# A planned four-layer kernel: convolution added up in PSUM, GpSimd's largest product in two, fillers for TensorE from the start

## The chip, the core and the metric

The kernel runs on one core of one Trainium2 chip. Its engines work from queues of their own: TensorE (PE; its weight loads are the row PEld), VectorE (DVE), ScalarE (ACT), GpSimd (POOL), and SyncE (SP), whose queue issues the DMAs. The metric is the time of one execution on the device in microseconds. The kernel before takes 1466.25 us (median of three runs, 1457.24 to 1469.72).

## What is computed

Four layers on x, which is 4 batches x 512 tokens x 256 features, all in float32, with a context of the same size. All the layers are wanted in this order:

```python
x = _L0_xattn_ref(x, ctx_1024, mask, ...)      # Mamba2 block, then cross-attention, 8 heads of 32
x = _L1_xattn_ref(x, ctx_1024, ctx_1024, ...)  # cross-attention, 8 heads of 16, and a feed-forward block
x = _L2_xattn_ref(x, ctx_1024, ...)            # cross-attention, 16 heads of 16, gelu
x = _L3_xattn_ref(x, ctx_1024, ...)            # cross-attention, 8 heads of 32, then a recurrence
```

The change touches two places of the Mamba2 block: the causal convolution over time with its silu, and the decay matrix of the scan.

```python
padded = jnp.pad(xBC, ((0, 0), (D_CONV - 1, 0), (0, 0)))
conv = conv_b + sum((padded[:, k:k + L, :] * conv_w[:, k] for k in range(D_CONV)))
xBC = jax.nn.silu(conv)
```

The recurrence at the end of layer 3 is serial over the 512 tokens, for all 4 batches at once, with a state of 64:

```python
def step(s, u_t):
    s = jax.nn.silu(s @ A.T) + u_t
    return (s, s)
```

## The kernel before

**Staging.** Tokens are worked on in four chunks of 128 (c = 0 to 3). A *front* per chunk does the Mamba2 block: projections, the convolution in six groups of 128 channels (`channels`), and a scan per batch (`scan`) that ends in an out-projection (`w_out`). Beside it, keys and values of all four layers are made from the context (`keys`, `slim_keys`, `values`, `of_weights`) and stored to HBM. When all of these are made, `with_keys_made` reuses their memory for the *wide* stream, the attention of layers 0 and 3 (tiles kw, vw, probs_w, turned_w), and loads its parameters. When all scans are done, `with_block_done` reuses the block's memory for the *slim* stream, layers 1 and 2 (tiles ks, vs, topped, probs_s), and loads sixteen parameters. Both streams reload keys and values from HBM for each job of one layer, chunk and batch.

**Rows.** Attention heads are 32 partitions wide, so four of them fit in TensorE's array side by side. A row slot is a group of matmuls that run at once in the array's row groups: two groups from one stream's half, and two more where another thread has a row ready (`rows`, `partner`). With no partner a slot uses half of the array.

**The end.** `from_layer3` makes the recurrence's input u (matmuls with wub). `recurrence` works in bank 7 of PSUM, which it takes for good: per chunk one matmul of u with amat, then per token a matmul into the step's four columns, a Tanh on ScalarE with a product on VectorE, or a Silu on ScalarE alone once all of the wide stream's exponentials are out (`exps["left"] == 0`).

**The planner.** Nothing of the order of work is written out by hand. Every operation is a step of a Python generator, a thread with an urgency; `Flow.run` keeps a planned clock of every engine with a cost for each operation, and emits again and again the operation that can begin first by that plan (a more urgent one if it can begin within 120 ns). What it emits stands in each engine's queue in that order and runs when its semaphores allow. So a change of one cost or one place moves all that follows. As every operation is recorded by the same line (`Op.emit`, line 127), the profile's groups show L127, and are told apart by their tiles.

PSUM has eight banks. `banks.single` gives the free bank whose last reader is planned to be done first, or None; `banks.give` returns one.

**Fillers.** `Flow.fill` looks, before TensorE's next operation, at the planned gap. If it is over 300 ns (GAP), it emits a matmul of ident with ident, whose result nobody reads, as wide as the gap allows, up to 256 columns. In the kernel before, `flow.filler` is set once the last second pass of the slim stream is emitted, so fillers stand only near the end: 184 of them, 168 after the recurrence's last input.

**The convolution.** In `channels`, a projection lands in one bank (px). It is copied to pad, behind the last three columns of the chunk before (halo). The fourth tap and the bias are an affine out of px into the tile xbc in SBUF, after which the bank is given back. Three products on VectorE (`scalar_tensor_tensor`) add the other taps, with both inputs and the output in SBUF. Then a Tanh on ScalarE and a last product make the silu.

**The decay matrix.** `scan` first makes lo, 128 x (8 x 128), as one GpSimd product of a triangle and the step's decay; later two halves of four heads are transformed and multiplied again.

Of the kernel before, what the change touches and what calls it, by code (L numbers as in the profile page):

```python
# [10 lines left out]
AF = mybir.ActivationFunctionType  # L11
ALU = mybir.AluOpType
# [3 lines left out]
P = 128  # L16
# [11 lines left out]
SD = 64  # L28
SZ = SD + 1
# [14 lines left out]
def over(ap, n):  # L44

    p, a = ap.shape
    return ap.unsqueeze(1).to_broadcast([p, n, a])
# [181 lines left out]
class Flow:  # L229
# [100 lines left out]
    def fill(self, e, start):  # L330

        while self.filler is not None and start - e.free > GAP:
            op = self.filler(min(256, int((start - e.free - 80) * 0.3) * 2))
            if op is None:
                return
            begin = max(e.free, self.there([op])) + DRAIN * (e.mode != op.mode)
            if begin + op.cost > start:
                return
            e.mode, e.free = op.mode, begin + op.cost
            op.emit()  # L340
            self.account([op], begin, e.free)
# [113 lines left out]
def tile_kernel(ctx: ExitStack, tc: tile.TileContext, a: dict, out: bass.AP):  # L455
# [509 lines left out]
    def front(c):  # L965
# [28 lines left out]
        def channels(ct):  # L994
            pad = yield Need(pads.take)
            bank = yield on_bank(lambda bank: project_t(ps[:, bank, :], w_in, xt, DI // P + ct))
            px = ps[:, bank[0], :].rearrange("p (b t) -> p b t", b=B)
            yield Until(lambda: halo_from[ct] == c - 1)
            yield G_.tensor_copy(pad[:, :, 0 : NCONV - 1], halo[:, ct])
            yield copy(pad[:, :, NCONV - 1 :], px)  # L1000
            acc = xbc[:, ct, :]
            acc_b = acc.rearrange("p (b t) -> p b t", b=B)
            yield affine(acc_b, px, conv_w[:, ct, NCONV - 1 : NCONV], conv_b[:, ct : ct + 1])
            banks.give(*bank)
            yield G_.tensor_copy(halo[:, ct], pad[:, :, P:])
            halo_from[ct] = c
            for k in range(NCONV - 1):
                yield V.scalar_tensor_tensor(
                    acc_b, pad[:, :, k : k + P], conv_w[:, ct, k : k + 1], acc_b,
                    ALU.mult, ALU.add,  # L1010
                )
            pads.give(pad)
            th = yield Need(ths.take)
            yield A.activation(th, acc, AF.Tanh)
            yield V.scalar_tensor_tensor(acc, th, 1.0, acc, ALU.add, ALU.mult)
            ths.give(th)
            todo["n"] -= 1

# [60 lines left out]
    def scan(c, i, xt, dt, da, dec, xbc, through):  # L1079
# [4 lines left out]
        state = states[i]  # L1084

        lo = yield Need(los.take)
        yield G_.tensor_tensor(lo, over(stri, NH), along(da[:, hh], P), ALU.mult)

        dbx = yield Need(dbxs.take)
        y = yield Need(ys.take)  # L1090
# [262 lines left out]

    us, rs = {}, {}
    fed = set()
    recurred = {"begun": 0, "multiplied": 0}

    def from_layer3(c, b, slot, ct):
        half = b // 2
# [22 lines left out]
    def recurrence():  # L1382
# [7 lines left out]
        for c in range(NT):  # L1390
            yield Until(lambda: {(c, 0), (c, 1)} <= fed)
            h, u, r = hs[c], us[c % 2], rs[c % 2]
            if c == 0:
                own = yield Need(banks.last)
                z = ps[0:SZ, own, :].rearrange("p (t b) -> p t b", b=B)
                yield G_.memset(u[:, :, 0:1], 0.0)
            else:
                yield G_.tensor_copy(u[:, :, 0:1], us[1 - c % 2][:, :, P : P + 1])
# [304 lines left out]
    def slim_second(lo):  # L1703

        for i in range(slim.all):
# [22 lines left out]
                yield from read_both(pr, lambda i, sc: A.activation(p[:, i, :], sc, AF.Exp))  # L1728
                slim_probs[n, lo] = p
            slim.keys_read(job)  # L1730
            if i == slim.all - 1:
                flow.filler = filler

    def slim_weigh():

# [55 lines left out]
        flow.add(job["after"](job["c"], job["b"], ct_slot, ct), CHAIN, f"from {job['l']} {job['c']}")  # L1791

    def filler(n):
        bank = banks.single()
        if bank is None:
            return None
        return mm(
            ps[0:SZ, bank[0], 0:n].rearrange("p (i t) -> p i t", i=2), ident[:, 0:SZ],
            over(ident[:, 0 : n // 2], 2),
        )  # L1800


    def with_keys_made():
# [147 lines left out]
```

## Time and profile before

| | |
|---|---|
| profiled execution | 1469.96 us, span 1468.2 us |
| median of three runs | 1466.25 us |
| mean granted TensorE clock | 0.964 |
| busy: PE, PEld, DVE | 1396.0, 990.9, 912.5 us |
| busy: ACT, POOL | 772.2, 229.8 us |
| fp32 matmul rows | 14656 for 8210 instructions: a float32 matmul is two rows, a transpose one |
| GpSimd's first product of lo, 128x1024 | 16 times, 1956 ns in the mean |
| VectorE's products of the convolution | 72 times, 832 ns in the mean |
| other products on VectorE, 128x512, one input in PSUM | 685 ns |
| filler of 202 columns | 354 ns a row in the mean with the other widths |

Times in the rows are taken by the hardware profiler from one execution. The ends of matmuls are modelled and follow each other in a pipeline, so that a busy TensorE need not be at its peak. In the waits, "A <- B x: t, n, l" means that A stood idle for t us, n times and at most l us, until B's work on x was done. The granted clock is the share of TensorE's full speed that the chip allowed in a stretch.

### The profile page before, as it was taken

The page shows a single profiled execution, that of the slowest core. Times are in us where ns is not written, and L with a number is a line of the kernel's source. Part 1 is how long each engine was busy: PE and PEld are TensorE (multiplying, and loading weights), DVE is VectorE, ACT ScalarE, POOL GpSimd, SP SyncE. Part 2 cuts the span into 40 slices and gives each one's busy share as a digit, 9 for nine tenths or more (in the row PEclk, how much of TensorE's full clock was granted, in tenths as well). Part 3 has the DMA queues.
Part 4 walks back from the last instruction along what each step waited for, and adds up shares of the span by engine and source line. Part 5 has one row for each costly group of instructions (what it writes and reads, how often), then busy time and mean ns, then how long its engine had stood idle before and what let it go on. Part 6 is the DMA issues. An engine that isn't in the chain of part 4 may idle for free.

```text
span 1468.2 us, 34894 instructions
## 1 busy us (share of the span) xinstructions
PE 1396.0 (95%) x14656; PEld 990.9 (67%) x14656; DVE 912.5 (62%) x2084; ACT 772.2 (53%) x1938; POOL 229.8 (16%) x369
## 2 busy tenths in 40 slices
PE   8999999989799999999999999999999999999999
PEld 5666767667475667776667676666767666677555
DVE  5777666666566677577675667666575666667100
ACT  4643434444464566566455656546666554577232
POOL 2244453544100011001010101001010000010000
PEclk9999999999899999899898899999999999999999
DMA  8331212200522122132121122221121231201000
GB/s 247 126 114 47 77 60 82 73 15 30 164 90 91 47 90 90 58 136 75 61 89 39 53 68 95 91 74 62 39 81 62 81 111 47 75 21 40 7 9 15
DMA packets 48245, 107.62 MB, mean 73 GB/s; under 512 B 12820, under 2 KB 24536, under 8 KB 48088
## 3 DMA queue, kind: packets, MB, share of 16 engines
q1 hardware_dynamic: 46584, 105.32, 21.6%
q8 instruction: 115, 1.88, 0.5%
q14 instruction: 42, 0.34, 0.1%
q10 hardware_dynamic: 1504, 0.07, 0.1%
HBM read 85.01 MB, written 20.37 MB: 72 GB/s over the span
## 4 chain that ended last, share of the span: by engine, by line
PE 85%; DVE 7%; ACT 5%; DMA 1%; issue 1%; SPq 0%; POOL 0%; DVEq 0%; ACTq 0%
PE ps L127 85%; DVE tops L127 3%; ACT probs_s L127 2%; DVE xbc L127 1%; ACT probs_w L127 1%; ACT L127 1%; DMA ks<-k 1%; ACT xt L127 0%; DVE h L127 0%; DMA ctx_in<-in_ctx 0%; DVE xt L127 0%; DVE stats L127 0%; DVE top L127 0%; DMA wq<-in_L_xattn_Wq 0%; DVE probs_w L127 0%
## 5 line engine op out<-in xcount | busy, mean ns | idle before, releaser
L127 DVE TENSOR_REDUCE tops<-ps 128x2 f32<-128x1024 f32 (+1 forms) x219 | 235.2, 1085 | 82.1 <-PE ps L127 81.5
L127 ACT ACTIVATE probs_s<-ps 128x1024 f32<-128x1024 f32 (+1 forms) x215 | 193.9, 929 | 101.6 <-PE ps L127 100.3
L127 PE MATMUL ps<-ks,queries 32*128 32x512 f32 x768 | 199.0, 670 | 17.5 <-DMA ks<-k 8.4
L127 PE MATMUL ps<-topped,ks 32*128 32x128 f32 x3072 | 192.4, 297 | 10.1 <-ACT rec_th L127 3.3
L127 PEld LDWEIGHTS ps<-topped,ks 32*128 32x128 f32 x3072 | 159.7, 197 | 35.2 <-issue 10.3
L127 PE MATMUL ps<-ident,probs_w 128*128 128x128 f32 x1024 | 139.8, 282 | 3.1 <-ACT probs_w L127 0.9
L127 PEld LDWEIGHTS ps<-rec,ahalf 65*65 65x65 f32 x656 | 72.9, 142 | 96.4 <-DVE rec L127 28.5
L127 PEld LDWEIGHTS ps<-ident,probs_w 128*128 128x128 f32 x1024 | 118.5, 146 | 20.6 <-issue 8.3
L127 ACT ACTIVATE rec_th<-ps 64x4 f32<-64x4 f32 x328 | 53.6, 163 | 127.2 <-PE ps L127 125.1
L127 ACT COPY turned_w<-ps 128x512 f32<-128x512 f32 x156 | 87.8, 585 | 56.2 <-PE ps L127 53.3
L127 PE MATMUL ps<-kw,queries 32*128 32x512 f32 x512 | 115.6, 641 | 0.8 <-DVE tops L127 0.8
L127 PE MATMUL ps<-probs_s,vs 128*32 128x128 f32 x3072 | 108.9, 283 | 0.7 <-ACT rec_th L127 0.7
L127 POOL COPY rb<-r 128x128 f32<-128x128 f32 x64 | 18.7, 292 | 570.0 <-DVE r L127 434.9
L127 ACT ACTIVATE probs_w<-ps,top 128x512 f32<-128x512 f32 x128 | 87.1, 684 | 27.0 <-DVE top L127 26.9
L127 PE MATMUL ps<-ident 128*65 128x202 f32 (+3 forms) x368 | 99.4, 354 | 0.1
L127 PE MATMUL ps<-rec,ahalf 65*65 65x4 f32 x656 | 88.6, 206 | 7.1 <-DVE rec L127 6.8
L127 ACT ACTIVATE probs_w<-probs_w,top 128x512 f32<-128x512 f32 x128 | 91.5, 717 | 5.4 <-DVE top L127 5.4
L127 PEld LDWEIGHTS ps<-probs_s,vs 128*32 128x32 f32 x3072 | 81.7, 113 | 16.1 <-issue 6.5
L127 DVE TENSOR_REDUCE top<-ps 128x2 f32<-128x1024 f32 (+1 forms) x70 | 78.5, 1125 | 18.3 <-PE ps L127 17.7
L127 DVE COPY turned_w<-ps 128x512 f32<-128x512 f32 x100 | 67.9, 688 | 34.6 <-PE ps L127 33.2
L127 DVE CUSTOM_DVE_ANT_0 probs_w<-ps,masked 128x512 f32<-128x512 f32 x128 | 84.0, 681 | 5.5 <-PE ps L127 5.5
L127 PEld LDWEIGHTS ps<-ks,queries 32*128 32x128 f32 x768 | 58.0, 191 | 41.1 <-issue 18.0
(227 smaller groups left out, 2441.3 us busy)
## 6 DMA issues: line engine op xcount, KB each, us to landing
ks<-k SPq DMA_DIRECT2D x48, 512.0 KB, 4.5
kw<-k SPq DMA_DIRECT2D x32, 512.0 KB, 3.5
vw<-v SPq DMA_DIRECT2D x32, 512.0 KB, 3.7
k<-k_out SPq DMA_DIRECT2D x20, 512.0 KB, 2.6
vs<-v SPq DMA_DIRECT2D x16, 574.0 KB, 3.8
vs<-v SPq DMA_DIRECT2D x16, 302.0 KB, 2.9
v<-v_out SPq DMA_DIRECT2D x8, 512.0 KB, 2.8
v<-v_out SPq DMA_DIRECT2D x4, 574.0 KB, 3.3
```

Source lines behind the costliest of these rows:

```text
L127: return getattr(self.engine.bass, self.name)(*self.args, **self.kw)
```

## The change

Three edits. First, the convolution stays in the projection's bank: the affine and the three products read and write px in place, Tanh reads the bank, the last product writes xbc, and only then the bank is given back. Second, the scan's first product is issued as two, of four heads each. Third, the filler is set before any work is planned, offers several widths, and, if no free bank's filler fits, offers a matmul into partitions 64 to 127 of bank 7 once the recurrence owns it. That last form is entered in the plan as writing nothing.

```diff
     def fill(self, e, start):
 
         while self.filler is not None and start - e.free > GAP:
-            op = self.filler(min(256, int((start - e.free - 80) * 0.3) * 2))
-            if op is None:
-                return
-            begin = max(e.free, self.there([op])) + DRAIN * (e.mode != op.mode)
-            if begin + op.cost > start:
+            n = min(256, int((start - e.free - 80) * 0.3) * 2)
+            for op in self.filler(n):
+                begin = max(e.free, self.there([op])) + DRAIN * (e.mode != op.mode)
+                if begin + op.cost <= start:
+                    break
+            else:
                 return
...
             yield copy(pad[:, :, NCONV - 1 :], px)
-            acc = xbc[:, ct, :]
-            acc_b = acc.rearrange("p (b t) -> p b t", b=B)
-            yield affine(acc_b, px, conv_w[:, ct, NCONV - 1 : NCONV], conv_b[:, ct : ct + 1])
-            banks.give(*bank)
+
+            yield affine(px, px, conv_w[:, ct, NCONV - 1 : NCONV], conv_b[:, ct : ct + 1])
             yield G_.tensor_copy(halo[:, ct], pad[:, :, P:])
             halo_from[ct] = c
             for k in range(NCONV - 1):
                 yield V.scalar_tensor_tensor(
-                    acc_b, pad[:, :, k : k + P], conv_w[:, ct, k : k + 1], acc_b,
-                    ALU.mult, ALU.add,
+                    px, pad[:, :, k : k + P], conv_w[:, ct, k : k + 1], px, ALU.mult, ALU.add
                 )
             pads.give(pad)
             th = yield Need(ths.take)
-            yield A.activation(th, acc, AF.Tanh)
-            yield V.scalar_tensor_tensor(acc, th, 1.0, acc, ALU.add, ALU.mult)
+            yield A.activation(th, ps[:, bank[0], :], AF.Tanh)
+            yield V.scalar_tensor_tensor(
+                xbc[:, ct, :], th, 1.0, ps[:, bank[0], :], ALU.add, ALU.mult
+            )
+            banks.give(*bank)
...
         lo = yield Need(los.take)
-        yield G_.tensor_tensor(lo, over(stri, NH), along(da[:, hh], P), ALU.mult)
+        for j in range(0, NH, 4):
+            h4 = slice(i * NH + j, i * NH + j + 4)
+            yield G_.tensor_tensor(lo[:, j : j + 4, :], over(stri, 4), along(da[:, h4], P), ALU.mult)
...
                 own = yield Need(banks.last)
+                recurred["own"] = True
...
-            if i == slim.all - 1:
-                flow.filler = filler
...
     def filler(n):
+
+        many = [n] + [m for m in (192, 128, 64) if m < n]
         bank = banks.single()
-        if bank is None:
-            return None
-        return mm(
-            ps[0:SZ, bank[0], 0:n].rearrange("p (i t) -> p i t", i=2), ident[:, 0:SZ],
-            over(ident[:, 0 : n // 2], 2),
-        )
+        if bank is not None:
+            for m in many:
+                yield mm(
+                    ps[0:SZ, bank[0], 0:m].rearrange("p (i t) -> p i t", i=2), ident[:, 0:SZ],
+                    over(ident[:, 0 : m // 2], 2),
+                )
+        if recurred["own"]:
+            for m in many:
+                op = mm(
+                    ps[SD:, 7, 0:m].rearrange("p (i t) -> p i t", i=2), ident[:, 0:SD],
+                    over(ident[:, 0 : m // 2], 2),
+                )
+                op.writes = []
+                yield op
...
+    flow.filler = filler
     flow.add(parameters(), CHAIN, "parameters")
```

More of the change, by code (lines that the diff above doesn't have):

```diff
@@ L1355, in tile_kernel @@
     fed = set()
-    recurred = {"begun": 0, "multiplied": 0}
+    recurred = {"begun": 0, "multiplied": 0, "own": False}
     def from_layer3(c, b, slot, ct):
```

## The prediction, made before the changed kernel ran

> **What bounds the kernel now.** I read the chain of waits first, then the slices, then who waits for whom on TensorE, then the granted clock in stretches of 50 and of 3 us.
>
> The chain of work that ended last, shares by engine:
>
> ```profile
> PE 85%; DVE 7%; ACT 5%; DMA 1%; issue 1%; SPq 0%; POOL 0%; DVEq 0%; ACTq 0%
> ```
>
> TensorE carries 85% of it. GpSimd, one of whose products the change splits, has 0%. The slices show how full TensorE is and what clock it was granted:
>
> ```profile
> PE   8999999989799999999999999999999999999999
> ...
> POOL 2244453544100011001010101001010000010000
> PEclk9999999999899999899898899999999999999999
> ```
>
> So there are three kinds of loss: idle TensorE (1468.2 - 1396.0 = 72 us), clock (mean 0.964, that is 0.036 x 1468 = 53 us of clock), and the end, where little work is left. The waits of TensorE (us in total, times, longest):
>
> ```profile
> PE ps L127 <- DMA ks<-k: 8.4, 1, 8.4
> ...
> PE ps L127 <- DMA ctx_in<-in_ctx: 6.7, 1, 6.7
> PE ps L127 <- DVE xbc L127: 5.5, 4, 2.8
> ```
>
> Up to 300 us TensorE waits for the convolution (xbc) only 0.8 us in one place; the other 4.7 us are at 315 to 320. The convolution's own rows, and the clock around one drop (3 us stretches; after the times: busy us of PE, PEld, DVE, ACT, POOL, then clock, DMA share, GB/s):
>
> ```profile
> L127 DVE SCALAR_TENSOR_TENSOR xbc<-pad,conv_w,xbc x72: 653/744/2346, 32.9 to 316.9; 128x512 f32<-128x512 f32 x72
> ```
>
> ```profile
> 606.00:609.00 3.00, 2.05 (x10) 0.70 (x6) 2.98 (x7) 0.00 (x0) 0.00 (x0) 0.80 0.00 0
> 609.00:612.00 3.00, 3.00 (x38) 2.78 (x36) 2.29 (x5) 0.18 (x1) 0.00 (x0) 0.50 0.00 0
> ```
>
> The clock falls to 0.50 for some 10 us although the idle piece just before is 0.95 us long. There are about 17 such drops, most between 400 and 1160 us. The end of the chain in order of time (start, us, what):
>
> ```profile
> 1366.84 21.55 PE ps L127 x160
> 1388.40 73.06 PE ps L127 x518
> ```
>
> The last input of the recurrence is ready at 1366.5 + 0.5; then 41 steps of chunk 2 run alone (21.4 us, 0.52 us a step), then the 128 of chunk 3.
>
> **The change part by part,** against the profiled execution (span 1468.2, execution 1469.96). Numbers on order come from the instruction order of the two built programs.
>
> *Convolution in PSUM.* Same 24 chains, same count. The 72 products took 832 ns in the mean against 653 at best: 72 x 0.18 = 13 us, and 24 x 0.13 = 3 us for the last step, lost where GpSimd held them up. The new form (one input and the output in PSUM) is in no row; nearest are 0.69 us (product with one PSUM input) and 0.81 (affine out of PSUM); I take 0.69, the same operation. ScalarE's affine written to PSUM is in no row either; I keep its 0.78. All of it is hidden behind TensorE, which runs matmuls back to back from 50 to 250 us (3.9 us idle). In return a chain holds its bank past its affine, through three products, tanh and the last step, 3 x 0.69 + 0.63 + 0.69 = 3.4 us longer, two of eight banks at a time; queued behind that are transposes and projections that want a bank. Price 0 to +5; TensorE waited 2.8 us for k_out, a bank's reader, so I take +1.
>
> *GpSimd's product in two.* 16 x 1956 ns become 32; the nearest row, a 128x512 product of the same form on dbx, takes 1081 ns, so +0.2 us a pair, 3.3 us in all. GpSimd is at most 57% busy (28.7 of 50 us at 250 to 300) and off the chain: 0. If that cover were gone, the scan's first matmuls with lo would be late by 0.2 us each time.
>
> *What both do to the order.* The out-projections of the mamba block end after 935 matmuls that are neither fillers nor steps, instead of 1125, while the first rows of the slim streams stay at 1168. Before, the 16 parameter loads stand in SP's queue ahead of the first keys with 43 matmuls to cover them, and TensorE waits 0.9 + 8.4 us. After, 233 cover them: about 104 transposes x 0.108, 18 matmuls x 0.43, 11 row slots x 1.1, 4 weighings x 1.08, some 35 us against 16 us of loading (376.3 to 392.1). With the 4.7 us for xbc that is -14. New is the hand-over: the wide stream now starts with no mamba work beside it. Before, 12.2 us lie between the last weight product (268.1) and the first possible wide row (280.3). Work for about 10 us is at hand there (12 + 8 matmuls x 0.43, 16 transposes x 0.108), then the first rows wait for their maximum and exponential, 4 us: +6, and +3 for a thinner stretch after it. Clock: the two old stalls cost about 8 us of it (0.93 and 0.90 in 300 to 400); I give back 6. Sum -11; ends -20 and +5.
>
> *Fillers at the start.* Nine, before the context lands at 6.7 us. The first 8 transposes took 1.94 us, later ones 1.04, and the matmuls behind them 4.68 instead of 3.7: up to -1.9, and up to +0.9 if the fillers run over. I take -1.
>
> *Fillers all along.* Before the last input of the recurrence there are 101 instead of 16: 9 at the start, 10 at the hand-over, 82 in between, 66 more there than before. At 198 columns one costs 198 x 1.67 ns = 0.33 us (a 256-column one 0.43 when packed). All of it on the path is +22, none is 0; TensorE idles 40 us between 400 and 1350, so I take a third, +7. What waits behind a filler is all of TensorE's queue: 40 of the 82 hold a semaphore wait of their own, 11 of them among the 18 that go beside the recurrence in bank 7. The gain is clock: 40 us of it are lost between 400 and 1350. 27 us of added activity against some 80 us at half clock: -12; ends 0 and -30.
>
> [...]
>
> *Row slots.* 302 instead of 296, those that use half of the array 92 instead of 80: 6 x 1.1 = +6.6.
>
> *The end.* 359 of 511 recurrence steps are multiplied before the last input instead of 342: 17 x 0.52 = -9. TensorE works in order, so this only fails if these steps hold it up earlier; ends -12 and 0.
>
> Sum: -11 + 1 - 1 + 7 - 12 + 6.6 - 9 = -18.4, so 1469.96 - 18.4 = 1451.6. The median of before, 1466.25, is 3.7 under its profiled execution: forecast 1448.
>
> **The rivals.**
> 1. *The clock comes back almost whole.* The drops are set off by little activity, and 82 fillers lift it nearly everywhere: -30 for -12, and none of them late. For it: the drops follow pieces of 0.5 to 1.2 us with one-sided rows and single steps. Against: at 258 to 264 the clock falls with TensorE busy throughout. 1448 - 18 = 1430.
> 2. *The fillers do nothing for the clock,* because the gaps that the schedule counts on are not where the chip has them, or because short gaps don't set the clock: the term of -12 is 0. 1448 + 12 = 1460. [...] The same time results if the new hand-over eats what the removed loading wait gives.
> 3. *Slower: fillers in the way of TensorE's queue, from 400 to 1366.* A filler that waits for a bank's reader, or in bank 7 for the step's own reader, starts when the real matmul could have started. All 66 then cost 0.33: +22 for +7; the clock gains nothing (+12) and twelve more one-sided slots bring about three more drops at 4 us (+12); the hand-over stays uncovered (+5). 1448 + 44 = 1492. With the clock term at 0 the sum passes zero once some 60% of the fillers lie on the path; from there the slots and the hand-over decide. For it: 40 waiting fillers. Against: in the last 73 us of before a filler stands between every two steps, and a step still takes only 0.56 us.
>
> **How the numbers follow.** A measurement of this kernel tells about 1% from no change (its three runs span 0.85%). Faster by more than that is below 1451.6, slower above 1480.9. Forecast 0.44 (its own range, plus and minus 14 for the bounds of the front and the fillers, 1434 to 1462: 0.30 faster, 0.14 same); rival 1 0.18 (faster); rival 2 0.16 (0.02 faster, 0.14 same); rival 3 0.22 (0.02 same, 0.20 slower). Faster 0.50, same 0.30, slower 0.20. The range leaves one tenth on each side: the good end takes in rival 1 and the favourable ends of the front (-9) and of the end (-3), 1418; the bad end takes in rival 2 with all fillers on the path (+15), 1475, and half of what rival 3 lies above that, 1484.
>
> **What would show it.** Right: no wait for ks near 380 us and slim rows at about 380 rather than 392; a bubble of 5 to 10 us at the hand-over; convolution products near 690 ns with hardly a spread; mean clock 0.97 to 0.98; last input to end 92 instead of 102 us. Wrong: a last input later than 1366 with the clock at 0.964 or less (rival 3 if fillers start right at the end of a wait; rival 2 if they lie in real gaps), or TensorE waiting for banks in the first 250 us.

## The result and the profile after

The changed kernel takes 1457.99 us (median of 22 runs, 1449.23 to 1463.28) against 1467.5 us for the kernel before in the same series (22 runs, 1455.82 to 1472.28): ratio 0.9944, 95% interval 0.9923 to 0.9964. It is faster by 0.56%, where 1.25% was forecast (1448 us); it lies inside the range. The profiled execution took 1461.58 us with a span of 1459.9, 8.3 us less than before. The kernel before runs in three groups of times, about 1457, 1464 and 1471 us with granted clocks of 0.974, 0.968 and 0.963, and its profiled execution is of the last group.

The page of the changed kernel: the chain's shares by engine, then the slices.

```profile
PE 87%; DVE 6%; ACT 5%; issue 1%; DMA 1%; POOL 0%; SPq 0%; DVEq 0%; ACTq 0%
```

```profile
PE   9999999999999999999999999999999999999999
...
PEclk9999999999999999999999999989999998999999
```

TensorE is over 90% busy in every slice now, and the five slices with a clock of 0.8 have become two. The waits of TensorE (us in total, times, longest):

```profile
PE ps L127 <- DVE top L127: 5.4, 5, 2.4
PE ps L127 <- ACT rec_th L127: 5.4, 12, 0.6
PE ps L127 <- DVE rec L127: 4.0, 8, 0.8
```

The three loading waits of the matmuls (ks 8.4, ctx_in 6.7, wq 0.9) and the 4.7 us for xbc are gone (fillers now run while ctx_in loads). The first rows of the slim streams start at 386 us, where 392 was the time before and about 380 the forecast. The new hand-over shows as a wait of a filler, in the timeline of TensorE (start, us, operation, in brackets the idle time before it and its releaser):

```profile
354.41 0.65 PE L127 MATMUL ps<-ident 128*65 128x256 f32 x2 [2.36 <-DVE top L127]
```

The products of the convolution (count: shortest/median/longest ns, first and last start) and the end of the chain:

```profile
L127 DVE SCALAR_TENSOR_TENSOR ps<-pad,conv_w,ps x72: 674/750/756, 31.6 to 258.1; 128x512 f32<-128x512 f32 x72
```

```profile
1365.51 12.79 PE ps L127 x94
...
1378.31 74.78 PE ps L127 x518
```

The products have lost their long ones (2346 ns before), and their median is about where it was (744). VectorE's step that makes the last input ready starts at 1365.2 us instead of 1366.5, and 24 steps of chunk 2 are left instead of 41. So of the 8.3 us, 7 are the end, and all that lies before it gave 1.3.

**An account of TensorE.** To see where the rest went I added up the matmul rows of each trace in the order of the instructions: the time from each start to the next, less the idle time in it, and less half of what lay in stretches with a granted clock of 0.50. That splits the span into a lead before the first matmul, *work* at full clock, *idle* time, the *loss* to the half clock (all three up to the last input), and the *end*. It comes to 3 us under the span in each kernel. In us:

| kernel | median | ratio | clock | lead | work | idle | loss | at half clock | end |
|---|---|---|---|---|---|---|---|---|---|
| before | 1467.5 | 1 | 0.964 | 6.7 | 1251.8 | 62.1 | 46.2 | 102 | 98.3 |
| changed | 1458.0 | 0.9944 | 0.975 | 1.4 | 1294.4 | 37.5 | 32.2 | 65 | 91.3 |
| e1 its order, fillers not issued | 1457.0 | 0.9937 | 0.977 | 7.3 | 1274.3 | 49.1 | 30.4 | 61 | 91.2 |
| e2 its order, fillers of 64 columns | 1465.3 | 0.9986 | 0.971 | 1.4 | 1280.5 | 47.7 | 38.6 | 79 | 91.3 |
| e3 edits 1 and 2 | 1468.3 | 1.0012 | 0.969 | 7.2 | 1272.4 | 52.3 | 42.4 | 85 | 95.5 |
| e4 edit 3 | 1447.9 | 0.9879 | 0.990 | 1.4 | 1297.4 | 45.0 | 11.1 | 27 | 86.8 |
| e5 order of e4, not issued | 1469.3 | 1.0033 | 0.966 | 7.3 | 1261.1 | 62.9 | 40.8 | 92 | 89.4 |
| e6 edit 1 | 1475.1 | 1.0072 | 0.968 | 7.3 | 1273.5 | 53.3 | 45.0 | 92 | 88.9 |
| e7 edit 2 | 1491.6 | 1.0186 | 0.956 | 6.9 | 1263.1 | 62.0 | 58.1 | 123 | 95.8 |
| e8 before, NEAR 125 | 1462.3 | 0.9978 | 0.968 | 6.8 | 1254.3 | 59.6 | 38.4 | 85 | 100.0 |
| e9 before, 65 fillers by count | 1461.9 | 0.9984 | 0.986 | 7.2 | 1286.0 | 53.2 | 14.9 | 34 | 99.9 |
| e10 the same over 33 rows | 1499.7 | 1.0242 | 0.958 | 7.3 | 1282.0 | 49.9 | 57.4 | 123 | 98.4 |
| e11 e5, fillers by count | 1469.5 | 1.0037 | 0.986 | 6.9 | 1296.6 | 56.5 | 15.2 | 34 | 89.5 |
| e12 e1, fillers by count | 1478.6 | 1.0103 | 0.978 | 6.9 | 1296.7 | 53.2 | 28.5 | 61 | 89.7 |
| e13 e4, fillers in bf16 | 1454.3 | 0.9959 | 0.975 | 1.3 | 1280.0 | 52.9 | 30.9 | 65 | 89.5 |
| e14 changed, fillers in bf16 | 1456.7 | 0.9958 | 0.974 | 1.3 | 1284.4 | 43.3 | 33.6 | 68 | 91.2 |
| e15 e4, half of the fillers | 1451.4 | 0.9919 | 0.983 | 1.4 | 1279.0 | 56.3 | 18.1 | 41 | 89.5 |
| e16 edits 1 and 3 | 1460.0 | 0.9961 | 0.974 | 1.4 | 1291.7 | 39.7 | 33.2 | 68 | 95.5 |
| e17 edits 2 and 3 | 1453.8 | 0.9899 | 0.988 | 1.4 | 1293.3 | 44.9 | 11.9 | 24 | 98.2 |
| e18 edit 3, NEAR 130 | 1436.2 | 0.9782 | 0.992 | 1.4 | 1286.4 | 42.0 | 8.9 | 21 | 91.1 |

Medians are of the timed runs, all else of one profiled execution each; ratios are against the kernel before on the same chip, worked out from all runs of both, and aren't the quotients of the medians. The profiled executions lie between 2.9 us under (e5) and 6.4 us over (e16) the median of their kernel, so small differences between rows of the account can be the execution's. From before to changed the work grew by 42.6 us: fillers 38.0, row slots 9.4, transposes -4.9, the rest 0. Idle time and lead fell by 29.9, the loss by 14.0, the end by 7.0.

### The profile page after: what moved, and what is told of

It is laid out like the page before. It is cut to its first block, busy times and chain, and to the rows that moved or that the text cites. A ratio compares the mean times of both kernels' runs of the same rounds, so it can differ in the third digit from the quotient of the medians.

```text
span 1459.9 us, 35245 instructions
## 1 busy us (share of the span) xinstructions
PE 1417.6 (97%) x14794; PEld 992.5 (68%) x14794; DVE 910.0 (62%) x2098; ACT 774.3 (53%) x1945; POOL 223.5 (15%) x385
## 4 chain that ended last, share of the span: by engine, by line
PE 87%; DVE 6%; ACT 5%; issue 1%; DMA 1%; POOL 0%; SPq 0%; DVEq 0%; ACTq 0%
PE ps L127 87%; ACT probs_s L127 2%; DVE tops L127 2%; DVE dt L127 1%; ACT L127 1%; DVE top L127 1%; DVE probs_w L127 1%; ACT probs_w L127 1%; DMA ctx_in<-in_ctx 0%; ACT xt L127 0%; ACT turned_w L127 0%; DVE turned_w L127 0%; DVE stats L127 0%; DVE xt L127 0%; DVE h L127 0%
## 5 line engine op out<-in xcount | busy, mean ns | idle before, releaser
L127 PE MATMUL ps<-topped,ks 32*128 32x128 f32 x3072 | 182.7, 296 | 4.9 <-ACT rec_th L127 1.4
L127 PEld LDWEIGHTS ps<-topped,ks 32*128 32x128 f32 x3072 | 150.9, 195 | 28.7 <-issue 11.8
L127 PE MATMUL ps<-ident 128*65 128x202 f32 (+16 forms) x506 | 135.4, 359 | 11.9 <-DVE top L127 4.6
L127 PE MATMUL ps<-ident,probs_w 128*128 128x128 f32 x1024 | 134.1, 276 | 0.4 <-ACT probs_s L127 0.2
L127 PE MATMUL ps<-kw,queries 32*128 32x512 f32 x512 | 124.9, 640 | 1.0 <-ACT rec_th L127 0.6
L127 PEld LDWEIGHTS ps<-ident,probs_w 128*128 128x128 f32 x1024 | 113.8, 142 | 15.5 <-ACT probs_w L127 5.0
L127 ACT COPY turned_w<-ps 128x512 f32<-128x512 f32 x162 | 91.6, 584 | 52.8 <-PE ps L127 49.1
L127 DVE CUSTOM_DVE_ANT_0 probs_w<-ps,masked 128x512 f32<-128x512 f32 x128 | 84.7, 681 | 18.2 <-PE ps L127 18.1
L127 PE MATMUL ps<-rec,ahalf 65*65 65x4 f32 x688 | 92.0, 204 | 0.4
L127 DVE SCALAR_TENSOR_TENSOR rec<-rec_th,ps 64x4 f32<-64x4 f32 x344 | 49.7, 144 | 67.5 <-ACT rec_th L127 62.9
L127 DVE COPY turned_w<-ps 128x512 f32<-128x512 f32 x94 | 63.8, 688 | 25.5 <-PE ps L127 24.0
```

What stands on the lines that cost most here:

```text
L127: return getattr(self.engine.bass, self.name)(*self.args, **self.kw)
```

## The experiments

Letters in an expectation stand for the theories that it names. "Before the end" means before the last second pass of the slim stream is emitted; the fillers after it were left as they are in every kernel. e1, e2, e5 and e9 to e15 change what is issued and not what is planned, so all other work keeps its order.

### The change taken apart: e1 to e8

**e1, fillers planned and not issued.**

```diff
-            op.emit()
+            if self.loud:
+                op.emit()
             self.account([op], begin, e.free)
```

> The changed kernel with its plan untouched, but the 80 fillers from the hand-over to the last input of the recurrence planned and not issued; the nine at the start are left out too, the ones at the end stay. So every other instruction stands in the same order. Three theories. A, fillers are paid for in full (TensorE's account of the changed kernel: 46 us of fillers before the last input against 6.5, idle 37 us against 62): without them TensorE idles about 25 us more, the clock falls from 0.975 to about 0.966, and the time stays within 0.3% of the changed kernel, ratio to before 0.992 to 0.997. B, the clock is worth it: slower than the changed kernel by 10 us or more, ratio 1.000 or above. C, they stand in the way: faster by 10 us or more, ratio 0.988 or below.

1457.03 us, ratio 0.9937 (0.9907 to 0.9966): the time of the changed kernel. Without its fillers the same order had 20 us less work (fillers -36, row slots +9, the rest +7) and 12 us more idle time and 6 of lead. The mean clock of the changed kernel and of e1:

```profile
core 0: 1459.9 us, clock 0.975
```

```profile
core 0: 1455.6 us, clock 0.977
```

A's time came out, but not its clock, which was to fall to 0.966; B and C fell. So in the order of the whole change the issued fillers are worth nothing, and what it gained over before came from the order.

**e2, fillers of 64 columns.** The same kernel with each filler before the end cut to 64 columns when issued.

```diff
-            op.emit()
+            (op if self.loud else self.thin(op)).emit()
```

> The same plan as the changed kernel, but each of the 101 fillers before the last input is issued with 64 columns instead of 198 in the mean (64-column fillers took 0.17 to 0.26 us of TensorE in the changed kernel's trace, the others 0.43 in the mean). A: some 20 us less of filling; if the clock stays near 0.975, TensorE waits instead for about two thirds of it and the ratio to before is 0.988 to 0.994; B: the clock needs the columns, falls to about 0.967, and the ratio is 0.996 or above. C, any filler delays by its own wait, not by its columns: the time stays as the changed kernel's, 0.994.

1465.31 us, ratio 0.9986 (0.9957 to 1.0014), clock 0.971. The 80 short fillers still take 18.6 us of work, 0.23 each, and the half clock grew to 79 us. The ratio is B's (0.996 or above), although B had fallen in e1; A's and C's are missed.

**e3, the first two edits without the third.**

```diff
-    flow.filler = filler
     flow.add(parameters(), CHAIN, "parameters")
```

> The changed kernel with the filler set where the kernel before sets it; 30 fillers before the last input, the rest at the end. Its plan is made anew: 303 row slots, 94 of them half empty, 351 recurrence steps before the last input (before: 296, 80, 342; changed: 302, 92, 359). Under A the gain of the changed kernel is made by the front (-6 us) and the end (9 steps, -5), less the row slots (+7): ratio about 0.997, clock about 0.966. Under B, without the fillers' clock, 1.003 or above. Under C 0.990 or below.

1468.3 us, ratio 1.0012 (0.9984 to 1.0041). Fewer stalls (idle -10) and 9 steps less at the end are eaten by 14 us more in row slots, 94 of them one-sided. The ratio lies between A's 0.997 and B's 1.003 and decides nothing.

**e4, the third edit alone.** The convolution and the GpSimd product as before.

```diff
-            if i == slim.all - 1:
-                flow.filler = filler
...
+    flow.filler = filler
     flow.add(parameters(), CHAIN, "parameters")
```

> The kernel before with the third edit alone (fillers from the start, several widths, bank 7); 115 fillers before the last input, 294 row slots, 76 half empty, 362 steps before the last input. A: the end gives -10 us (20 steps), the fillers and the clock cancel, the loading wait near 380 us stays: ratio 0.991 to 0.995, clock about 0.975. B: 0.985 or below. C: above 1.000.

1447.85 us, ratio 0.9879 (0.9836 to 0.9922): faster than the whole change. The loss fell from 46 to 11 us. The ratio lies between A's and B's; A's clock of 0.975 is missed.

**e5, the order of e4 without the fillers** (the edit of e1).

> The third edit alone gave 1447.9 us (ratio 0.988, granted clock 0.990). This kernel keeps that kernel's order of all other work, and doesn't issue the fillers that lie before the last input of the recurrence (those at the end stay). P (the order that the planner lays out anew sets time and clock, the issued fillers are worth nothing): 1444 to 1452 us, ratio 0.985 to 0.991, clock 0.98 or more. C (the half clock follows windows of 3.41 us in which TensorE idles for about 1 us or more, and the issued fillers empty those windows): idle before the last input rises from 45 to about 60 us, half-clock time from 27 to about 70 us, 1455 to 1464 us, ratio 0.993 to 0.998, clock about 0.970.

1469.31 us, ratio 1.0033 (0.9998 to 1.0068). The mean clock of e4 and of e5:

```profile
core 0: 1444.8 us, clock 0.990
```

```profile
core 0: 1464.7 us, clock 0.966
```

Here the fillers are worth 1.5%: 44 us of filler work against 24 us of idle time and lead, and 30 us of loss. C's time for this kernel was 1455 to 1464; it came out slower, with 92 us at half clock where C had about 70, and P fell. But e1 and e5 are the same edit with opposite results, so "fillers raise the clock" was not yet an explanation.

**e6 and e7, the first and the second edit alone.**

```diff
-        yield G_.tensor_tensor(lo, over(stri, NH), along(da[:, hh], P), ALU.mult)
+        for j in range(0, NH, 4):
+            h4 = slice(i * NH + j, i * NH + j + 4)
+            yield G_.tensor_tensor(lo[:, j : j + 4, :], over(stri, 4), along(da[:, h4], P), ALU.mult)
```

(e7; e6 has the convolution of the change, and near the end the widths that the new filler offers.)

> The kernel before with the first edit alone (the convolution added up in the bank). Both first edits together gave 1468.3 us (ratio 1.0012). Theory G (the convolution's edit brings the front's gain, the split takes it back): 1455 us, ratio 0.992, with the split alone above 1470. Theory N (neither brings anything; what a slim row's slots and an order laid out anew give and take covers both): 1462 to 1473 us, ratio 0.997 to 1.004. In both, the convolution's products take 690 to 760 ns without any over 800.

> The kernel before with the second edit alone (GpSimd's largest product in two). G: above 1470 us, ratio 1.003 or more. N: 1462 to 1473 us, ratio 0.997 to 1.004. The convolution's products on VectorE keep their longest ones over 2 us under both if it is not the size of GpSimd's product that delays them, and fall under 1.3 us if it is.

e6: 1475.1 us, 1.0072 (1.0033 to 1.0112), with products of 675 to 756 ns. e7: 1491.55 us, 1.0186 (1.0138 to 1.0235). Neither theory had a loss from the first edit. e6 has 22 us more work, 12 of it in row slots, against 9 us less idle time and 9 at the end. In the two profiles e6 is only 3 us longer, where the ratio means about 10, so its loss is only in part accounted for. e7 moved the end of the out-projections from 1125 to 1166 matmuls: no idle time less, 11 us more work and 12 us more loss. GpSimd's own rows in e7:

```profile
L127 POOL TENSOR_TENSOR lo<-stri,dt x32: 1034/1040/1489, 67.4 to 351.2; 128x512 f32<-128x512 f32 x32
```

and the longest convolution product fell from 2346 to 1752 ns. The split did what it says, on an engine that has 0% of the chain of before.

**e8, another order and nothing else.**

```diff
-NEAR = 120.0
+NEAR = 125.0
```

> The kernel before with none of the edits, but with the planner's limit NEAR at 125 instead of 120, which only makes it lay out part of the work in another order (72 lone row slots instead of 80). P (any new order moves the time by about as much as the whole change did): beyond 0.3% of the kernel before to either side, that is below 1462 or above 1471 us; by the 8 slots x 1.1 us alone it would be 1458 us. S (an order laid out anew is worth nothing by itself): 1463 to 1470 us, ratio 0.997 to 1.002, clock 0.962 to 0.966.

1462.33 us, ratio 0.9978 (0.9948 to 1.0008): 7 us less by the median, but the interval of the ratio takes in no difference. It leaves P and S undecided; e18 comes back to it.

### What the half clock followed: e9, e10 and the count

In the clock records of before and of the changed kernel 26 stretches at half clock begin and end inside the trace: 8 of 3.413 us, 13 of 6.827, three of 10.240, one of 13.653 and one of 17.067. Those at full clock between them are whole multiples of 3.413 us as well, to 2 ns, so each of the two traces can be cut into one grid of stretches of 3.413 us. In 7 of the 26 cases TensorE was idle for less than 0.1 us in the stretch just before. One of the 7, in the changed kernel (stretch; busy us and rows of PE, PEld, DVE, ACT, POOL; clock; DMA share and GB/s), and TensorE's timeline in it:

```profile
1223.90:1227.30 3.40, 3.40 (x18) 2.24 (x16) 2.98 (x8) 0.22 (x2) 0.00 (x0) 1.00 0.03 5
1227.30:1230.70 3.40, 3.40 (x20) 1.38 (x18) 3.40 (x5) 0.43 (x3) 0.00 (x0) 1.00 0.00 0
1230.70:1234.10 3.40, 3.40 (x10) 1.13 (x10) 2.38 (x6) 0.24 (x2) 0.00 (x0) 0.50 0.00 0
```

```profile
1227.75 0.28 PE L127 MATMUL ps<-rec,ahalf 65*65 65x4 f32 x2
1227.96 1.13 PE L127 MATMUL ps<-ks,queries 32*128 32x512 f32 x4
1229.02 0.28 PE L127 MATMUL ps<-rec,ahalf 65*65 65x4 f32 x2
1229.23 1.13 PE L127 MATMUL ps<-ks,queries 32*128 32x512 f32 x4
```

Busy 3.40 of 3.40 us, and the next stretch runs at 0.50. What fills it are one-sided row slots, 32 rows each in two of the four row groups, and steps of 4 columns. That suggested counting how much of the array works rather than whether TensorE is busy: per matmul row of the trace, columns x rows / 128, spread over its time, and summed over each 3.413 us of the grid. A 256-column filler (two rows of the trace, 0.43 us) counts 512; a one-sided slot counts 512 in 1.1 us (a slot over all four groups took 1.14 us, at 1220.53 us of the changed kernel), so three of them and the steps between them come to about 1500.

I formed this from the traces of before, changed and e1 to e8; e9 to e18 were not there yet. It is a count over the twenty traces of this kernel and its variants; they don't show how the chip decides. Stretches at full clock, and how many of them the half clock follows:

| count in the stretch | first ten traces | followed | e9 to e18 | followed |
|---|---|---|---|---|
| under 1500 | 115 | 113 | 81 | 80 |
| 1500 to 1600 | 34 | 10 | 18 | 7 |
| over 1600 | 3847 | 5 | 3966 | 2 |

The columns of bf16 in e13 and e14 are counted as one half, which was chosen from those two traces (below).

Idle time sorts them far worse: of all 8061 stretches the best single limit on the count (1531) puts 19 on the wrong side, the best limit on idle time 182, and a count that leaves the transposes out 202. Of the 165 stretches (all twenty traces) with over 1 us idle, 90 are followed; 82 of those 90 have a count under 1500, and of the 72 with a count over 1600 only 3 are followed. Of the 47 with under 0.2 us idle and a count under 1500, 46 are followed. 1500 is 1500 / 512 x 0.43 = 1.26 us of the whole array, 37% of the stretch. At half clock the same count goes with what follows: of 175 stretches at half clock with a count under 1500, 174 are followed by another; of 236 over 1600, 32 are. A one-sided slot took 1.13 us at full clock and 2.08 at half clock (1227.96 and 1233.15 us of the changed kernel), so in a stretch at half clock the same work counts about half.

**e9 and e10** test it with the order of before. At places that the trace of before shows as thin (count below 1600 in 3.41 us at any phase) stand 65 fillers of 256 columns, over 128 rows in e9 and over 33 in e10. AT maps the number of a TensorE instruction to the fillers after it (the first entry is shown); they go to bank 7 or to a free bank.

```diff
+AT = {375: 1,
...
+        if e.kind == "PE" and e.after is not None:
+            e.n += 1
+            for _ in range(AT.get(e.n - 1, 0)):
+                e.after(self)
```

```diff
-                dst.rearrange("p (i t) -> p i t", i=2), ident[:, 0 : dst.shape[0]],
-                over(ident[:, :], 2),
+                dst.rearrange("p (i t) -> p i t", i=2), ident[0:33, 0 : dst.shape[0]],
+                over(ident[0:33, :], 2),
```

> The kernel before with its order of all work kept, and 65 fillers of 256 columns by 128 rows put by the position of the instruction, where the trace of before shows stretches of 3.41 us with little work for the array, counted as columns x passes x rows/128. R (the clock halves in the window after one whose count is below about 1530, idle or not; the ten traces so far have 118 of 120 windows below 1516 followed by the half clock and 10 of 3876 above): half-clock time before the last input falls from 102 us to 20 to 40 us, which gives back 30 to 38 us of the 46 us lost to it; the fillers take 65 x 0.43 = 28 us, of which about 10 lie in idle time: 1443 to 1456 us, ratio 0.983 to 0.992, clock 0.983 or more. I (idle time of 1 us and more brings the half clock, busy time of any kind prevents it): only what falls into idle time counts, half-clock time 70 to 90 us, 1462 to 1480 us. Q (the fillers stand in the way): above 1475 us.

> The same kernel as the one before in this list, with the same fillers at the same places and of the same columns, but over 33 rows instead of 128, which takes TensorE as long and counts a quarter. R: half-clock time stays at 75 to 105 us, the fillers' 28 us less some 10 of idle time are paid for without a return: 1472 to 1490 us, ratio 1.003 to 1.015, clock 0.962 to 0.973. I: the same time and clock as with 128 rows, to 0.3%.

e9: 1461.88 us, 0.9984 (0.9956 to 1.0011). e10: 1499.72 us, 1.0242 (1.0206 to 1.0277). The groups of TensorE between 400 and 1350 us by form show that the fillers take the same time (busy us, mean ns of one, idle before), then the slices of the clock, each for e9 and for e10:

```profile
L127 PE MATMUL ps<-ident 128*64 128x256 f32 x86 | 26.3, 414 | 0.2 <-ACT rec_th L127 0.2
```

```profile
L127 PE MATMUL ps<-ident 33*64 33x256 f32 x86 | 27.2, 424 | 0.2 <-ACT rec_th L127 0.2
```

```profile
PEclk9999999999899999999999999999999999999999
```

```profile
PEclk9999999989899999899999899899989999999999
```

Same order, same places, same columns, same occupancy; only the rows differ, and the half clock before the last input goes from 102 us to 34 in the one and to 123 in the other. That is 2.6% in time. I, by which busy time of any kind would do, is refuted. R's clock held in e9; in e10 it fell further than R had it (123 us at half clock against 75 to 105, 0.958 against 0.962 to 0.973). R's time held in neither: e9 was to take 1443 to 1456. Its fillers added 34 us of work, 0.53 each instead of 0.43, and found 9 us of idle time, so they cost nearly what the clock gave back (31 us of loss). e10 lies above R's range: its fillers, too, took 34 us, and it has 20 us more half clock than before without any. Fillers that count a quarter may push other work out of a stretch; no run shows that by itself.

**e11 and e12, fillers by the count in the orders of e5 and e1:** the edit of e9, with AT from the traces of these two (65 and 52 fillers).

> The order of the third edit alone, without its fillers before the last input (1469.3 us, clock 0.966), and 65 fillers of 256 columns put by the position of the instruction where that trace shows a count below 1600 in 3.41 us. R: main part +18 us of filler and shift, half-clock time from 92 to 20 to 40 us (loss 41 to 9 to 18 us): 1445 to 1460 us, ratio 0.985 to 0.996, clock 0.983 or more. I: half-clock time 60 to 80 us, 1465 to 1480 us.

> The order of the changed kernel without its fillers before the last input (1457.0 us, clock 0.977), and 52 fillers of 256 columns put by the position of the instruction where that trace shows a count below 1600 in 3.41 us. The change's own 80 to 100 fillers left 65 us of half-clock time there, about as much as without them. R: 52 x 0.43 = 22 us of filler, 15 us of it on the path; half-clock time from 61 to 15 to 35 us (loss 30 to 8 to 17 us): 1448 to 1460 us, ratio 0.987 to 0.995, clock 0.983 or more. I: half-clock time 50 to 65 us, 1462 to 1475 us.

e11: 1469.49 us, 1.0037 (1.0005 to 1.0069): half clock 92 to 34 us as R had it, and again all of it paid for in work (+35), so that R's time, 1445 to 1460, was missed. Planned into gaps, the fillers of e4 cost 44 us of work and take 18 of idle time and 6 of lead with them; placed by hand, 35 against 6. e12: 1478.6 us, 1.0103 (1.0066 to 1.0139), a miss of R: the half clock stayed at 61 us, in the range of theory I. Stretch by stretch the count holds in e12 too: each of its 8 stretches at full clock with less than 1500 is followed by the half clock. Its thin stretches lie elsewhere than in the trace that they were placed by, several in rows of three or four that begin with 1 us of idle time and then stay at half clock.

### How cheap a filler can be, and which edit holds the change back: e13 to e18

**e13 and e14, the fillers in bf16,** one pass over twice the columns, from a tile of ones made at the start.

```diff
+                op.real = mm(
+                    ps[0:SZ, bank[0], 0 : 2 * m].rearrange("p (i t) -> p i t", i=2),
+                    lit[:, 0:SZ], over(lit[:, 0:m], 2),
+                )
```

> The order of the third edit alone (1447.9 us, clock 0.990), each filler before the end issued as one pass of bf16 over twice the columns (512 instead of 256) instead of two passes of f32: the same columns x passes, and by one pass instead of two about half the time or less. S (columns x passes x rows count, whatever the type): half-clock time before the last input stays at 20 to 45 us; the fillers' 44 us fall to 20 or less, part of it comes back as idle time: 1430 to 1443 us, ratio 0.975 to 0.985, clock 0.983 or more. T (the array's time counts): half-clock time 50 to 90 us, 1445 to 1462 us, clock 0.968 to 0.980.

> The changed kernel (1458 us, clock 0.975; 65 us of half clock with its fillers, 61 without) with its fillers before the end as one pass of bf16 over twice the columns. S: half-clock time as with the f32 fillers, 45 to 70 us, and 10 to 16 us less of TensorE's time on the path: 1442 to 1450 us, ratio 0.983 to 0.989. T: half-clock time 60 to 80 us, 1450 to 1460 us.

e13: 1454.34 us, 0.9959 (0.993 to 0.9987). e14: 1456.68 us, 0.9958 (0.993 to 0.9985). The fillers of e13 take 26.5 us instead of 44 and leave 65 us of half clock instead of 27: T, the array's time counts. e14 lies in T's ranges, too. The two traces have 21 stretches at full clock with such fillers in them and less than 1530 from all else. If a bf16 column counts one half, those that the half clock follows all lie under 1530 and all others over it; if it counts one, about half of those followed lie over it. So here a filler bought clock by its time on the array, and a faster one bought less.

**e15, only the fillers that the count asks for.** The planner keeps the count of its own last 3.41 us.

```diff
-            op.emit()
+            if self.loud or self.lately(e.free) < NEED:
+                op.emit()
```

> The order of the third edit alone, fillers before the end issued only where the plan's own count of columns x passes x rows/128 of the last 3.41 us is below 1800 (57 of 115 are left). If the count is what matters, the 58 others bought nothing but idle time: half-clock time 20 to 45 us, 58 x 0.43 = 25 us less of fillers, some 60% of it on the path: 1432 to 1446 us, ratio 0.976 to 0.988. If the fillers' number matters: half-clock time about 60 us, 1455 to 1462 us.

1451.36 us, 0.9919 (0.989 to 0.9948): no gain over e4. The half clock (41 us) is as the first theory had it, the time lies between both. 25 us less of fillers came back as 11 us of idle time, 7 of loss and 7 of other work.

**e16 and e17, the third edit with the first and with the second:** the changed kernel with GpSimd's product whole again (e16), and with the convolution in SBUF again (e17).

> The changed kernel with the second edit (GpSimd's product in two) undone: first and third edit. The first alone gave 1475 us (1.0072), the third alone 1447.9 (0.988), both and the second 1458 (0.9944). If the first edit's loss (12 us more in slim rows, at full clock) stays beside the fillers: 1452 to 1462 us, ratio 0.991 to 0.997. If the second edit is what takes the gain back: 1440 to 1448 us.

> The changed kernel with the first edit undone: second and third edit. If the second edit's loss alone (24 us) stays beside fillers: about 1470 us, ratio 1.000 to 1.010. If most of that loss is the clock of its order (58 us lost to the half clock against 46 before), which fillers give back: 1445 to 1458 us, ratio 0.985 to 0.995. Its order has 72 lone row slots against 80 before and 349 steps before the last input against 342.

e16: 1460.01 us, 0.9961 (0.9925 to 0.9998), in the range of its first theory. e17: 1453.77 us, 0.9899 (0.9861 to 0.9938), in that of its second. With these the table of the three edits is whole (ratios to before):

| | neither | edit 1 | edit 2 | 1 and 2 |
|---|---|---|---|---|
| without edit 3 | 1 | 1.0072 | 1.0186 | 1.0012 |
| with edit 3 | 0.9879 | 0.9961 | 0.9899 | 0.9944 |

Of these eight only the kernels with the third edit are faster than before. In the whole change that gain comes through the order that the planner lays out with it, since e1 keeps the time without the fillers. The edits don't add up: the first costs 0.7 to 0.8% where the second is absent; beside the second it gains 1.7% without the third edit and costs 0.5% with it. Of what the second costs alone, about half is clock in the trace (12 us of loss, 11 of work), and with the third edit that loss is gone (58 us in e7, 12 in e17).

**e18, the third edit in another order.**

```diff
-NEAR = 120.0
+NEAR = 130.0
```

> The third edit alone with the planner's limit NEAR at 130 instead of 120: another order, with 68 lone row slots instead of 76, 354 steps instead of 362 before the last input and 104 fillers instead of 115. By 8 x 1.1 us less in row slots, 8 x 0.52 us more at the end and 2 us less of fillers: 7 us under the third edit alone, 1441 us, with the clock at 0.985 to 0.990: 1436 to 1447 us, ratio 0.980 to 0.988. If the order's luck with the clock outweighs that: 1450 to 1462 us.

1436.23 us, 0.9782 (0.9747 to 0.9817), 22 us under the changed kernel. Its clock, slices and end:

```profile
core 0: 1432.9 us, clock 0.992
```

```profile
PEclk9999999999999999999999999999999999999999
```

```profile
1338.68 15.51 PE ps L127 x114
1354.19 71.93 PE ps L127 x518
```

The last input is ready 27 us earlier than in the changed kernel and more steps are left after it (the last 128 take 71.9 us, at full clock throughout). Against e4 the work is 11 us less (fillers 6, rows 4), idle 3, loss 2, and the end 4 us longer. It was chosen among 17 settings of the planner's limits for its few one-sided slots, 68, and fewer fillers; how much of the gain is that and how much the luck of one order, one such kernel doesn't tell.

## Why the prediction was right in sign and off in size

The terms of its sum beside the account, in us:

| term | forecast | measured |
|---|---|---|
| stalls, hand-over, thinner stretch, banks, start, mid fillers: work of fillers less idle time | +2 | +8.1 (fillers 38.0, idle and lead -29.9) |
| clock, front and middle | -18 | -14.0 |
| row slots | +6.6 | +9.4 |
| transposes and the rest of the work | 0 | -4.9 |
| the end | -9 | -7.0 |
| sum | -18.4 | -8.4 |

- *The step that failed* is the fillers' gain of clock: "27 us of added activity against some 80 us at half clock: -12". e1 is the same order without these fillers. Over all runs the median granted clock is 0.978 with them and 0.977 without; in the traces the loss to the half clock is 32.2 us with them and 30.4 without, and after the 1300th matmul of real work (406.5 us in the changed kernel) 25 with them and 17 without. So the term of -12 came out as no gain at all. With +7 for their price and -1 for the start the sum had the fillers at -6; against e1 they came to +1 us by the ratios, with about 5 us to either side, and to +4 in the two spans.
- *The price* beside it, "I take a third, +7", was not far off. After the 1300th matmul fillers took 25 us more than in e1. 10 us of that came out of idle time, and 11 out of time that the other matmuls took longer without them, which leaves 4. Against the kernel before it looks dearer (27 us of fillers, 0.43 each instead of 0.33, for 14 of idle time), but that comparison has the other order in it.
- *The rest of the sum*, the order without the fillers, was to give -12.4 (-11 + 1 + 6.6 - 9), and e1 has a span 12.6 us under before's (9 us by the ratio). That is luck in part: in e1 row slots took 19 us more instead of 6.6, the loss fell by 16 instead of 6, and idle time and lead by 12 where the front's terms had 5. The ks, wq and xbc waits went as forecast, and so did the bubble at the hand-over (5 us of idle TensorE in e1 from 340 to 362 us), but at the 1300th matmul e1 is 2 us behind before and the changed kernel 6.6 us ahead, where the sum had 11.
- *The clock* rose as forecast (0.975, inside 0.97 to 0.98), and by luck: e1 has it without the fillers. "Added activity" names the right quantity, since in e9 and e10 the same fillers left 34 us at half clock over 128 rows and 123 over 33, and in another order such fillers lifted the clock (0.990 in e4 against 0.966 in e5). Why they didn't in this one is open. At full clock and over all phases of the grid, the order of e1 has 13.8 thin stretches (a count under some 1525) and the changed kernel 8.0; the kernel before has 14, so the clock that e1 gained over it isn't explained by their number either. In the traces of e1 and of the changed kernel 12 episodes became 8, but of 8.1 us each instead of 5.1, among them 17.1 us at 944 and 13.7 us at 1231, where one-sided slots follow each other and the plan sees no gap to fill. Whether that length is chance of the phase, one trace of each can't tell; it stays open.
- *The end* went as forecast. That TensorE works in order shows in the trace of before: 14128 of its 14656 matmul rows stand at their place in the built program, and the other 528 are 32-row matmuls of row slots. 17 steps fewer are left and gave 8.7 us of work; a longer stretch at half clock in the end took 1.7 of it.
- *The convolution* was to take 690 ns a product; it takes 750 in the median, near the 744 of before, hidden either way. In before, the 48 products with no GpSimd operation beside them took 734 to 752 ns, and each of the seven longer ones had one beside it; in the changed kernel 45 have one and none is over 756. The wait for a bank didn't show (k_out 0.9 us instead of 2.8). Row slots, priced at +6.6, took 9.4 us more; e6, which has the first edit alone, has 12 of that kind.
- *Rival 1* (clock almost whole, 1430) is not this kernel; e4 and e18 come near it, with clocks of 0.990 and 0.992 at 1448 and 1436 us. *Rival 2* (1460) came out: the time is near it, and the fillers did nothing for the clock here, as e1 shows. Of its reasons, that short gaps don't set the clock fits the count, but it can't be all, as e4 shows (0.990 against 0.966 in e5). Long gaps went with the half clock: after the start the twenty traces have 13 idle gaps over 3 us (one of 8.4 us at 383 us of before), and at each the half clock is granted, in three of them from just before the gap. But in these traces the half clock came without such a gap too: of 47 stretches with hardly any idle time and a low count 46 were followed by the half clock, and of 72 with over 1 us idle and a count over 1600 only 3. *Rival 3* (1492) is refuted: the kernel is faster than before, and in e1 taking the fillers away gained nothing.

## What to carry to other kernels

Look at where the granted clock falls and count there what the array does, rows x columns, before filling idle time: here TensorE lost its clock while busy (46 of 47 stretches with under 0.2 us idle and a count under 1500 were followed by the half clock), as at 1227 us of the changed kernel, where one-sided slots had 64 rows at work. A filler costs TensorE its own time (0.43 us in the mean in the changed kernel), and here it paid in one order (e4, 1.5% under e5) and not in another (the changed kernel and e1, the same time); over fewer rows it bought no clock (0.958 in e10 against 0.986 in e9), and in bf16 less (0.975 in e13 against 0.990 in e4). With a planner that lays out all later work anew, run every edit alone and each order with and without its fillers: another order with the same edit (e18 against e4) moved the time by 1.0%, more than the whole change did.

## What was not expected of the hardware

- In the twenty traces the half clock follows a count, in stretches of 3.413 us: under 1500 columns of float32 passes over 128 rows (1.26 us of the array) 193 of 196 stretches are followed by the half clock, over 1600 7 of 7813.
- 16 matmuls of one column over 128 rows (mean, nctx) fill 2 us of TensorE with almost no count: the clock falls at 260 us of before with TensorE busy throughout, after a stretch with them whose count is 1471.
- A float32 filler of 256 columns takes as long over 33 rows as over 128 (424 and 414 ns a row of the trace in the mean), and 65 of them over 33 rows leave the kernel 2.6% slower than 65 over 128.
